# The last feed-forward in groups of two batches, with its convolution as diagonal products on TensorE

## The chip, the cores and the metric

The kernel runs on one core of a Trainium2 chip. A core has five engines that work side by side, each through its own instructions in a fixed order: TensorE (PE; loading its stationary operand is shown apart as PEld), VectorE (DVE), ScalarE (ACT), GpSimd (POOL) and SyncE (SP), which here issues most transfers. They wait for each other by semaphores. PE reads SBUF and writes PSUM, which has eight banks[...]. The metric is the device time of one execution in microseconds (us); the median of several runs is taken.

## The reference

The program is two layers over x of 8 batches x 112 tokens x 256 channels. Each layer adds a cross-attention and a feed-forward to x, both on normalised x. The first feed-forward is a mixture of experts. The second one, which is changed, is a feed-forward with quantised activations and ternary weights, and a convolution of three taps along the tokens:

```python
def act_quant(x):
    scale = 127.0 / jnp.clip(jnp.max(jnp.abs(x), axis=-1, keepdims=True), 1e-05)
    return jnp.clip(jnp.round(x * scale), -128, 127) / scale
...
h = bit_linear(x, w1)                            # 256 -> 1024 channels
h = depthwise_conv1d(h.transpose(0, 2, 1), conv_w, conv_b)
h = h.transpose(0, 2, 1)
h = jax.nn.silu(h)
return bit_linear(h, w2)                         # 1024 -> 256
```

bit_linear quantises its input for each token (act_quant over all channels) and its weight to -1, 0 and 1 times a mean. So the second quantisation needs, for every token, the largest magnitude over 1024 channels after SiLU.

## The kernel before, in words

The kernel is written in a language in which tiles are taken from pools of rotating buffers, and a scheduler orders the instructions of each engine when the program is built, by readiness and by place in the program. All waits are made from the tiles' uses. A pool opened after another was closed takes over its memory.

The stages follow each other: attention of layer 0 with the routing, the experts (to about 449 us), attention of layer 1 (`attention(1, ...)`, L843), and the last feed-forward (L846 to L953). Attention 1 begins with `combine` (L507), which gathers the experts' results by 16 indirect transfers issued on POOL (L511). It ends with `project` for the last batch (L669), whose addition to x (L674) the feed-forward waits for. Attention 1 uses all eight PSUM banks, and its SBUF pools lie where the feed-forward's pools come to lie. The experts' weights were in a pool `wexp` that is closed before attention 1 (L839).

The feed-forward works on two halves of four batches each, 448 tokens (`HT`).

- `quantize_in` (L878): normalises four batches (`ln_apply`, L217), takes each token's largest magnitude (L883), forms scale and step (`quant_scales`, L855), multiplies and clamps (L887, L890), rounds by adding and subtracting a large constant `MAGIC` (L890, L891), transposes on PE (L896) with copies on ACT (L897). The step of each token is laid along the free axis of all partitions by `spread` (L865): a diagonal is made on DVE (L868) and multiplied by ones on PE (L875); dT (L899) is its copy.
- `conv` (L902), once for each of eight blocks of 128 channels (`NF`): two bf16 products (L907) into one bank, h on DVE as product times dT (L911), the middle tap and bias on ACT (L913), the two outer taps on DVE (L914, L917), SiLU on ACT (L920) into `ys`.
- `quantize_out` (L923): the largest magnitude over the eight blocks in one reduction (L925), across the partitions by transposes (L930) and a second reduction (L932), scales, `spread` of the scale, multiplication (L935), clamping (L936), rounding to bf16 (L938), and for each batch eight bf16 products (L943), scaling with the addition of x (L947), and the output transfer on SP's queue (L948).

Both halves' inputs come first, then both convolutions, then both outputs (L950 to L953), unless the scheduler finds an engine free.

Of the kernel before, what the change touches and what calls it, by code (L numbers as in the profile page):

```python
# [12 lines left out]
F32 = mybir.dt.float32  # L13
BF16 = mybir.dt.bfloat16
I32 = mybir.dt.int32
AF = mybir.ActivationFunctionType
ALU = mybir.AluOpType
# [6 lines left out]
H, A = 16, 16  # L24
E, F = 8, 1024
NF = F // 128
HB = B // 2
HT = HB * S
G = 4


# [23 lines left out]
def xattn_ffn_kernel(  # L55
# [17 lines left out]
    def const(shape, name, dt=F32):  # L73
        return cp.tile(shape, dt, tag=name, name=name)
# [28 lines left out]
    def col(name, j=0, n=1):  # L103
        lo = COLS[name][0] + j
        return colt[:, lo : lo + n]
# [49 lines left out]
    vbuf = [kp.tile([KC, NKC, H, 2 * A], F32, tag="v", name="v") for _ in range(3)]  # L155
    for v in vbuf:
        nc.gpsimd.memset(v, 1.0)
    desc = const([128, E], "desc")
    first = const([128, E], "first")
    for e in range(E):  # L160
# [54 lines left out]
    def ln_apply(dst, b, stats):  # L215
        mv, rs = stats
        nc.vector.tensor_scalar(dst, xs[b], mv[:, 0:1], rs, ALU.subtract, ALU.mult)  # L217
# [28 lines left out]
    class Router:  # L246
        def __init__(self, pool, misc, small):
            self.pool, self.misc, self.small = pool, misc, small
            self.cproj = const([128, 2, E], "cproj")
            self.cn = const([128, E], "cn")  # L250
            self.cn1 = const([128, E], "cn1")
# [28 lines left out]
        def norm(self, b, stats):  # L280
            n = self.pool.tile([S, D], F32, tag="r_n", name="rn")
            ln_apply(n, b, stats)
            return n
# [472 lines left out]
    with (  # L756
# [50 lines left out]
        def back(t, hT):  # L807
            w2, b2 = experts[t][1][:, : NF * D].rearrange("p (f d) -> p f d", f=NF), experts[t][1][:, NF * D :]
            py = ps_y.tile([TP, D], F32, tag="y", name="t_y")
            for f in range(NF):  # L810
                nc.tensor.matmul(py, hT[:, f, :], w2[:, f, :], start=(f == 0), stop=(f == NF - 1))  # L811
            y = f3.tile([TP, D], F32, tag="y", name="y")
            nc.vector.tensor_tensor(y, py, b2, ALU.add)  # L813
            return y
# [23 lines left out]

    held.close()  # L839


    stats_f1 = {}
    attention(1, {}, stats_f1)  # L843


    with (  # L846
        tc.tile_pool(name="ffn", bufs=2) as fp,
        tc.tile_pool(name="ffn3", bufs=3) as f3,
        tc.tile_pool(name="ffn1", bufs=1) as f1,
        tc.tile_pool(name="fps_h", bufs=3, space=PSUM) as ps_h,  # L850
        tc.tile_pool(name="fps_y", bufs=2, space=PSUM) as ps_y,
        tc.tile_pool(name="fps_m", bufs=2, space=PSUM) as ps_m,
    ):

        def quant_scales(peak, mean, nb):  # L855

            s = fp.tile([S, nb], F32, tag="qs", name="qs")
            d = fp.tile([S, nb], F32, tag="qd", name="qd")
            nc.vector.tensor_scalar_max(peak, peak, 1e-5)
            nc.vector.reciprocal(s, peak)  # L860
            nc.vector.tensor_scalar_mul(s, s, 127.0)
            nc.vector.tensor_scalar(d, peak, 1.0 / 127.0, mean[:S], ALU.mult, ALU.mult)
            return s, d

        def spread(per_token):  # L865

            dg = fp.tile([S, HB, S], F32, tag="diag", name="diag")
            nc.vector.tensor_tensor(  # L868
                dg,
                ident[:S, :S].unsqueeze(1).to_broadcast([S, HB, S]),  # L870
                per_token.unsqueeze(2).to_broadcast([S, HB, S]),
                ALU.mult,
            )
            t = ps_m.tile([128, HT], F32, tag="m", name="t_sp")
            nc.tensor.matmul(t, ones[:S, :], dg.rearrange("p b s -> p (b s)"), start=True, stop=True)  # L875
            return t

        def quantize_in(i):  # L878
            nall = fp.tile([S, HB, D], F32, tag="nall", name="nall")
            for bb in range(HB):  # L880
                ln_apply(nall[:, bb, :], i * HB + bb, stats_f1[i * HB + bb])
            peak = fp.tile([S, HB], F32, tag="peak", name="peak")
            nc.vector.tensor_reduce(peak, nall, AX.X, ALU.max, apply_absolute_value=True)  # L883
            s, d = quant_scales(peak, w1mean, HB)
            q = fp.tile([S, HB, D], BF16, tag="q16", name="q16")
            for bb in range(HB):
                nc.vector.tensor_scalar(  # L887
                    nall[:, bb, :], nall[:, bb, :], s[:, bb : bb + 1], 127.0, ALU.mult, ALU.min
                )
            nc.vector.tensor_scalar(nall, nall, -128.0, MAGIC, ALU.max, ALU.add)  # L890
            nc.vector.tensor_scalar_sub(q, nall, MAGIC)  # L891
            qT = fp.tile([128, 2, HT], BF16, tag="qT", name="qT")
            for bb in range(HB):
                t = ps_m.tile([128, 2, S], BF16, tag="m", name="t_q")
                for c in range(2):
                    nc.tensor.transpose(t[:, c, :], q[:, bb, c * 128 : (c + 1) * 128], ident16[:S, :S])  # L896
                nc.scalar.copy(qT[:, :, bb * S : (bb + 1) * S], t)  # L897
            dT = fp.tile([128, HT], F32, tag="dT", name="dT")
            nc.vector.tensor_copy(dT, spread(d))  # L899
            return qT, dT  # L900

        def conv(qT, dT):  # L902
            ys = fp.tile([128, NF, HT], F32, tag="ys", name="ys")
            for f in range(NF):
                t = ps_h.tile([128, HT], F32, tag="h", name="t_h")
                for c in range(2):
                    nc.tensor.matmul(  # L907
                        t, w1q[:, c, f * 128 : (f + 1) * 128], qT[:, c, :], start=(c == 0), stop=(c == 1)
                    )
                h = f3.tile([128, HB, S], F32, tag="h", name="h")  # L910
                nc.vector.tensor_tensor(h.rearrange("p b s -> p (b s)"), t, dT, ALU.mult)  # L911
                y = f3.tile([128, HB, S], F32, tag="y", name="y")
                nc.scalar.activation(y, h, AF.Identity, bias=col("cb", f), scale=col("cw", 3 * f + 1))  # L913
                nc.vector.scalar_tensor_tensor(  # L914
                    y[:, :, 1:S], h[:, :, 0 : S - 1], col("cw", 3 * f), y[:, :, 1:S], ALU.mult, ALU.add
                )
                nc.vector.scalar_tensor_tensor(  # L917
                    y[:, :, 0 : S - 1], h[:, :, 1:S], col("cw", 3 * f + 2), y[:, :, 0 : S - 1], ALU.mult, ALU.add
                )
                nc.scalar.activation(ys[:, f, :], y.rearrange("p b s -> p (b s)"), AF.Silu)  # L920
            return ys

        def quantize_out(i, ys):  # L923
            am = fp.tile([128, HT], F32, tag="am", name="am")
            nc.vector.tensor_reduce(  # L925
                am, ys.rearrange("p f t -> p t f"), AX.X, ALU.max, apply_absolute_value=True
            )
            t = ps_m.tile([S, HB, 128], F32, tag="m", name="t_am")
            for bb in range(HB):
                nc.tensor.transpose(t[:, bb, :], am[:, bb * S : (bb + 1) * S], ident)  # L930
            peak = fp.tile([S, HB], F32, tag="peak", name="peak")
            nc.vector.tensor_reduce(peak, t, AX.X, ALU.max)  # L932
            s, d = quant_scales(peak, w2mean, HB)
            sT = spread(s)
            nc.vector.tensor_tensor(ys, ys, sT.unsqueeze(1).to_broadcast([128, NF, HT]), ALU.mult)  # L935
            nc.vector.tensor_scalar(ys, ys, 127.0, -128.0, ALU.min, ALU.max)  # L936
            q = fp.tile([128, NF, HT], BF16, tag="yq", name="yq")
            nc.vector.tensor_scalar(q, ys, MAGIC, MAGIC, ALU.add, ALU.subtract)  # L938
            for bb in range(HB):
                b = i * HB + bb  # L940
                t = ps_y.tile([S, D], F32, tag="y", name="t_y")
                for f in range(NF):
                    nc.tensor.matmul(  # L943
                        t, q[:, f, bb * S : (bb + 1) * S], w2q[:, f, :], start=(f == 0), stop=(f == NF - 1)
                    )
                o = fp.tile([S, D], F32, tag="o", name="o")
                nc.vector.scalar_tensor_tensor(o, t, d[:, bb : bb + 1], xs[b], ALU.mult, ALU.add)  # L947
                nc.sync.dma_start(out=out[b], in_=o)  # L948

        ins = [quantize_in(i) for i in range(2)]  # L950
        ys = [conv(*ins[i]) for i in range(2)]
        for i in range(2):
            quantize_out(i, ys[i])  # L953


_ORDER = [
# [72 lines left out]
```

## Time and profile before

| What | Value |
|---|---|
| Time, median of 3 runs | 776.65 us (776.01 to 777.24) |
| The profiled execution's own time | 783.55 us |
| Its span, first to last instruction | 781.8 us |
| PE, DVE, ACT, POOL busy over the span | 656.6, 461.5, 240.9, 43.2 us |
| Mean granted TensorE clock | 0.862 |
| From 690 us to the end: PE, DVE, ACT busy | 32.3, 76.8, 23.4 us |
| Last x complete (L674 starts) | 690.0 us |
| Last output computed (L947 starts) | 778.2 us |

A group's line reads: line of the kernel, engine, operation, output tile <- input tiles, shapes (partitions x elements; for PE first the rows x columns of the array), count | busy us, mean ns of one | idle us of the engine before them, and what ended most of it. A timeline's line reads: start, duration, engine, line, operation, tiles, count, and in brackets the idle time before. Busy time of PE is modelled at its end, since matmuls are pipelined: several in a row take less than the sum of their means. An fp32 matmul in the program shows as two instructions. The granted clock is TensorE's share of full speed; it is recorded as 0.5 or 1.0, and a mean lies between.

### The profile page before, as it was taken

Reading aid. Unit: us, or ns where it says so; the run is one execution under the profiler, and the core shown is the slowest. Engines: PE = TensorE matmul, PEld = TensorE weight load, DVE = VectorE, ACT = ScalarE, POOL = GpSimd, SP = SyncE. Lnnn points to the kernel's source line nnn. Section 1 sums busy time; section 2 is a strip of 40 time slices with the busy share of each in tenths; the row PEclk is TensorE's granted clock in tenths of the full one; section 3 lists DMA queues with packets and bytes.
Section 4 is the critical chain, followed back from the end, with each engine's and each line's share of the span. In section 5 each row is a group of like instructions: output and inputs, shape, how many; then the busy total and the mean of one; then the engine's idle time right before and its main releaser. Section 6 shows DMA issues by size and latency. Waiting matters only on the chain.

```text
span 781.8 us, 15060 instructions
## 1 busy us (share of the span) xinstructions
PE 656.6 (84%) x5906; PEld 473.8 (61%) x5906; DVE 461.5 (59%) x1664; ACT 240.9 (31%) x476; POOL 43.2 (6%) x83
## 2 busy tenths in 40 slices
PE   4999989999989739999999967999999989845143
PEld 2666666566556529999999844666666656621032
DVE  8855677765763750111011148769887886479975
ACT  1124333233233214433434311133433332317300
POOL 4000000000000110000000061000000000000000
PEclk9999999999688959999999986579999986556558
DMA  9999101002000016979899420000000000000001
GB/s 298 366 344 347 68 2 55 13 14 68 14 13 13 26 57 242 317 279 354 330 328 358 160 83 19 1 2 1 2 2 2 2 1 2 1 1 0 0 10 37
DMA packets 37074, 82.73 MB, mean 106 GB/s; under 512 B 3228, under 2 KB 29196, under 8 KB 31628
## 3 DMA queue, kind: packets, MB, share of 16 engines
q1 hardware_dynamic: 34092, 76.25, 27.7%
q0 software_dynamic: 1536, 3.67, 1.5%
q10 hardware_dynamic: 1376, 1.87, 0.8%
q8 instruction: 46, 0.75, 0.4%
q14 instruction: 24, 0.20, 0.1%
HBM read 61.59 MB, written 20.19 MB: 105 GB/s over the span
## 4 chain that ended last, share of the span: by engine, by line
PE 66%; DVE 20%; DMA 6%; issue 4%; ACT 2%; SPq 1%; POOL 0%; another core or an unknown queue 0%; POOLq 0%; DVEq 0%; ACTq 0%
PE t_k L229 10%; PE t_h L800 10%; PE t_y L811 9%; PE t_p L618 7%; PE sc L585 7%; PE po L640 5%; PE t_v L236 4%; PE t_q L535 4%; DMA tok<-rn,at 2%; PE t_out L673 2%; DVE am L925 2%; PE t_o L652 2%; DVE a L198 1%; DVE top L588 1%; PE t_y L943 1%
## 5 line engine op out<-in xcount | busy, mean ns | idle before, releaser
L229 PE MATMUL t_k<-ctx,wk 128*128 128x375 f32 x256 | 96.3, 520 | 4.3 <-DMA ctx<-in_ctxT_dram 3.5
L800 PE MATMUL t_h<-tnT,we 128*128 128x128 f32 x672 | 92.1, 281 | 0.5 <-DMA we<-in_WA_dram 0.3
L800 PEld LDWEIGHTS t_h<-tnT,we 128*128 128x128 f32 x672 | 87.8, 194 | 7.4 <-ACT hT L804 1.6
L585 PE MATMUL sc<-k,q 32*112 32x375 f32 x512 | 86.9, 576 | 4.4 <-DVE pT L628 2.3
L804 ACT ACTIVATE hT<-t_h,we 128x128 f32<-128x128 f32 x168 | 61.4, 368 | 91.9 <-PE t_h L800 86.4
L811 PE MATMUL t_y<-we,hT 128*128 128x256 f32 x336 | 82.8, 380 | 0.0
L618 PE MATMUL t_p<-qa,k 32*125 32x112 f32 x1536 | 78.9, 315 | 2.9 <-DVE top L588 1.5
L630 ACT ACTIVATE pT<-pT 125x672 f32<-125x672 f32 x64 | 48.8, 763 | 105.5 <-DVE pT L628 103.4
L618 PEld LDWEIGHTS t_p<-qa,k 32*125 32x125 f32 x1536 | 62.6, 209 | 20.8 <-issue 14.0
L588 DVE TENSOR_REDUCE top<-sc 112x2 f32<-112x750 f32 x64 | 57.9, 933 | 26.7 <-PE sc L585 26.6
L229 PEld LDWEIGHTS t_k<-ctx,wk 128*128 128x128 f32 x256 | 49.1, 203 | 35.3 <-issue 6.1
L630 ACT ACTIVATE pT<-t_p 125x672 f32<-125x672 f32 x64 | 43.3, 728 | 86.0 <-PE t_p L618 85.9
L628 DVE TENSOR_TENSOR pT<-t_p,maskT 125x336 f32<-125x336 f32 x128 | 56.6, 499 | 21.4 <-PE t_p L618 21.4
L595 DVE CUSTOM_DVE_ANT_0 sm<-sc,mask 112x375 f32<-112x375 f32 x128 | 63.0, 541 | 9.8 <-PE sc L585 9.7
L640 PE MATMUL po<-pT,v 125*32 125x112 f32 x1536 | 62.4, 288 | 6.7 <-ACT pT L630 4.3
L811 PEld LDWEIGHTS t_y<-we,hT 128*128 128x128 f32 x336 | 59.1, 191 | 5.5
L640 PEld LDWEIGHTS po<-pT,v 125*32 125x32 f32 x1536 | 41.1, 119 | 31.3 <-ACT pT L630 13.5
L789 DVE COPY tnT<-t_tn 128x256 f32<-128x256 f32 x21 | 8.9, 425 | 78.0 <-PE t_tn L787 70.7
L813 DVE TENSOR_TENSOR y<-t_y,we 128x256 f32<-128x256 f32 x21 | 8.9, 424 | 68.9 <-PE t_y L811 68.8
L585 PEld LDWEIGHTS sc<-k,q 32*112 32x112 f32 x512 | 29.1, 189 | 31.5 <-issue 17.0
L236 PE MATMUL t_v<-wv,ctx 128*125 128x256 f32 x192 | 45.9, 387 | 0.3 <-ACT k L558 0.3
L535 PE MATMUL t_q<-nT,wq 128*128 128x112 f32 x256 | 37.7, 308 | 3.1 <-DVE qa L608 2.5
(207 smaller groups left out, 772.4 us busy)
## 6 DMA issues: line engine op xcount, KB each, us to landing
we<-in_WB_dram SPq DMA_DIRECT2D x21, 1152.0 KB, 7.8
we<-in_WA_dram SPq DMA_DIRECT2D x21, 1028.0 KB, 6.6
tok<-zero SPq DMA_DIRECT2D x8, 896.0 KB, 9.7
ysc<-zero SPq DMA_DIRECT2D x8, 896.0 KB, 10.7
ctx<-in_ctxT_dram SPq DMA_DIRECT2D x8, 375.0 KB, 7.3
tn<-tok SPq DMA_DIRECT2D x21, 128.0 KB, 7.0
ysc<-y SPq DMA_DIRECT2D x21, 128.0 KB, 3.6
we<-in_w1T_dram SPq DMA_DIRECT2D x1, 1024.0 KB, 9.3
```

The lines of the kernel that those rows point to most:

```text
L229: nc.tensor.matmul(t, wts[layer]["k"][:, c, g * 128 : (g + 1) * 128], ctx_t[b][:, c, :], start=(c == 0), stop=(c == 1),)
L236: nc.tensor.matmul(t, ctx_t[b][:, c, i * KC : (i + 1) * KC], wts[layer]["v"][:, c, :], start=(c == 0), stop=(c == 1),)
L535: nc.tensor.matmul(t[:, g, :], wts[layer]["q"][:, c, g * 128 : (g + 1) * 128], nT[:, c, :], start=(c == 0), stop=(c == 1),)
L585: nc.tensor.matmul(ts[j // 2][:S, j % 2, :SK], q[r, g, :], k[r, g, :], start=True, stop=True)
L588: nc.vector.tensor_reduce(top[:, g, 2 * m : 2 * m + 2, A : A + 1], ts[m][:S, :, :SK], AX.X, ALU.max, negate=True,)
L595: nc.vector.tensor_tensor_reduce(out=sm, in0=ts[m][:S, i, :SK], in1=mask_t, scale=-1.0, scalar=3.0e38, op0=ALU.add, op1=ALU.min, accum_out ...
L618: nc.tensor.matmul(ts[j // 2][:KC, j % 2, c * S : (c + 1) * S], k[r, g, c * KC : (c + 1) * KC], qa[r, g, :], start=True, stop=True,)
L630: nc.scalar.activation(pT, src, AF.Exp)
L640: nc.tensor.matmul(po[32 * j : 32 * j + 32, g, :], v[:, c, 4 * g + j, :], pTs[j // 2][:, j % 2, c * S : (c + 1) * S], start=(c == 0), stop ...
L800: nc.tensor.matmul(ph[:, i, :], w1[:, c, f * 128 : (f + 1) * 128], nt[:, c, :], start=(c == 0), stop=(c == 1),)
L804: nc.scalar.activation(hT[:, f, :], ph[:, i, :], AF.Gelu, bias=b1[:, f : f + 1])
L811: nc.tensor.matmul(py, hT[:, f, :], w2[:, f, :], start=(f == 0), stop=(f == NF - 1))
```

## The change

The feed-forward is put into a class `Ffn` that works on four groups of two batches (`GB` = 2, 224 tokens, `GT`), with its own tiles.

- Input: `norm`, `quant` and `turn_in` do for two batches what `quantize_in` did for four. Clamps are left out; scaling and adding `MAGIC` are one DVE instruction, and subtracting it with rounding to bf16 is an ACT instruction (`minus_magic` as bias). dT is copied on ACT. The diagonals of `spread` are made on POOL.
- Convolution: for two channel blocks at once, four bf16 products fill one bank, and DVE writes h into one of three padded buffers `hpad` (zeros at both ends of each batch). Each tap is then an fp32 product of a 128x128 diagonal matrix of tap weights (`taps`) with the shifted h, three adding up in PSUM for each block, 96 in all. ACT applies SiLU with the convolution's bias straight from PSUM.
- Largest magnitude: ACT takes Abs of each pair of blocks, DVE keeps a running maximum; `peaks` finishes it.
- Output: `back` is as before without clamping, for two batches, and is placed within the next group's convolution.
- `late`, called after attention 1 in the program, fills `hpad` with zeros and makes `taps` on POOL. Their pool is opened before attention 1, in the memory of `wexp`.
- PSUM: two banks for first products (`ps_h`), three for taps (`ps_c`), three for the rest (`ps_m`).

```diff
-HB = B // 2
-HT = HB * S
+GB = 2
+GT, NGR = GB * S, B // GB
...
+    minus_magic = const([128, 1], "mmagic")
+    nc.gpsimd.memset(minus_magic, -MAGIC)
...
+    lp = ctx.enter_context(tc.tile_pool(name="late", bufs=1))
+    hpad = [lp.tile([128, 2, GB, S + 2], F32, tag=f"hpad{i}", name=f"hpad{i}") for i in range(3)]
+    taps = lp.tile([128, NF * 3, 128], F32, tag="taps", name="taps")
+
+    def late():
+        for t in hpad:
+            nc.gpsimd.memset(t, 0.0)
+        for f in range(NF):
+            nc.gpsimd.tensor_tensor(
+                taps[:, 3 * f : 3 * f + 3, :],
+                ident.unsqueeze(1).to_broadcast([128, 3, 128]),
+                col("cw", 3 * f, 3).unsqueeze(2).to_broadcast([128, 3, 128]),
+                ALU.mult,
+            )
...
     attention(1, {}, stats_f1)
+    late()
...
-        tc.tile_pool(name="fps_h", bufs=3, space=PSUM) as ps_h,
-        tc.tile_pool(name="fps_y", bufs=2, space=PSUM) as ps_y,
-        tc.tile_pool(name="fps_m", bufs=2, space=PSUM) as ps_m,
+        tc.tile_pool(name="fps_h", bufs=2, space=PSUM) as ps_h,
+        tc.tile_pool(name="fps_c", bufs=3, space=PSUM) as ps_c,
+        tc.tile_pool(name="fps_m", bufs=3, space=PSUM) as ps_m,
...
+            def spread(self, per_token):
+                e = self.p2.tile([S, GB, S], F32, tag="diag", name="diag")
+                nc.gpsimd.tensor_tensor(
+                    e,
+                    ident[:S, :S].unsqueeze(1).to_broadcast([S, GB, S]),
+                    per_token.unsqueeze(2).to_broadcast([S, GB, S]),
+                    ALU.mult,
                 )
+                t = self.bank_m("t_sp")[:, :GT]
+                nc.tensor.matmul(t, ones[:S, :], e.rearrange("p b s -> p (b s)"), start=True, stop=True)
+                return t
...
+            def quant(self, g):
+                n = self.st[g].pop("n")
+                peak = self.p2.tile([S, GB], F32, tag="peak", name="peak")
+                nc.vector.tensor_reduce(peak, n, AX.X, ALU.max, apply_absolute_value=True)
+                s, d = self.scales(peak, w1mean)
+                q = self.p2.tile([S, GB, D], BF16, tag="q16", name="q16")
+                for bb in range(GB):
+                    nc.vector.tensor_scalar(n[:, bb, :], n[:, bb, :], s[:, bb : bb + 1], MAGIC, ALU.mult, ALU.add)
+                nc.scalar.activation(q, n, AF.Identity, bias=minus_magic[:S])
+                self.st[g]["q"], self.st[g]["d"] = q, d
...
+            def conv(self, g, fp, silu):
...
+                t = self.bank_h("t_h")[:, : 2 * GT].rearrange("p (i n) -> p i n", i=2)
+                for i in range(2):
+                    f = 2 * fp + i
+                    for c in range(2):
+                        nc.tensor.matmul(
+                            t[:, i, :], w1q[:, c, f * 128 : (f + 1) * 128], st["qT"][:, c, :],
+                            start=(c == 0), stop=(c == 1),
+                        )
+                h = hpad[self.turn % 3]
+                self.turn += 1
+                nc.vector.tensor_tensor(
+                    h[:, :, :, 1 : S + 1], t.rearrange("p i (b s) -> p i b s", b=GB),
+                    st["dT"].rearrange("p (b s) -> p b s", b=GB).unsqueeze(1).to_broadcast([128, 2, GB, S]),
+                    ALU.mult,
+                )
+                y = self.bank_c("t_c")[:, : 2 * GT].rearrange("p (i b s) -> p i b s", i=2, b=GB)
+                for i in range(2):
+                    f = 2 * fp + i
+                    for j in range(3):
+                        nc.tensor.matmul(
+                            y[:, i], taps[:, 3 * f + j, :], h[:, i, :, j : j + S], start=(j == 0), stop=(j == 2)
+                        )
+                for i in range(2):
+                    f = 2 * fp + i
+                    nc.scalar.activation(
+                        st["ys"][:, f, :].rearrange("p (b s) -> p b s", b=GB), y[:, i],
+                        AF.Silu if silu else AF.Identity, bias=col("cb", f),
                     )
+                if silu:
+                    self.magnitudes(g, fp)
+
+            def magnitudes(self, g, fp):
+                st = self.st[g]
+                ys = st["ys"][:, 2 * fp : 2 * fp + 2, :]
+                a = self.p2.tile([128, 2, GT], F32, tag="am" if fp == 0 else "ab", name="am")
+                nc.scalar.activation(a, ys, AF.Abs)
+                if fp == 0:
+                    st["am"] = a
+                else:
+                    nc.vector.tensor_tensor(st["am"], st["am"], a, ALU.max)
...
+            def peaks(self, g):
+                m = self.st[g].pop("am")
+                nc.vector.tensor_tensor(m[:, 0], m[:, 0], m[:, 1], ALU.max)
+                t = self.bank_m("t_am")[:S, : GB * 128].rearrange("s (b p) -> s b p", b=GB)
+                for bb in range(GB):
+                    nc.tensor.transpose(t[:, bb, :], m[:, 0, bb * S : (bb + 1) * S], ident)
+                peak = self.p2.tile([S, GB], F32, tag="peak", name="peak")
+                nc.vector.tensor_reduce(peak, t, AX.X, ALU.max)
+                s, self.st[g]["d"] = self.scales(peak, w2mean)
+                self.st[g]["sT"] = self.spread(s)
+
+            def back(self, g):
+                st = self.st[g]
+                ys = st.pop("ys")
+                nc.vector.tensor_tensor(ys, ys, st.pop("sT").unsqueeze(1).to_broadcast([128, NF, GT]), ALU.mult)
+                q = self.p2.tile([128, NF, GT], BF16, tag="yq", name="yq")
+                nc.vector.tensor_scalar(q, ys, MAGIC, MAGIC, ALU.add, ALU.subtract)
...
+        begin(0)
+        for g in range(NGR):
+            for f in range(NF // 2):
+                ff.conv(g, f, True)
+                if f == 1 and g + 1 < NGR:
+                    begin(g + 1)
+                if f == 2 and g > 0:
+                    ff.back(g - 1)
+            ff.peaks(g)
+        ff.back(NGR - 1)
```

`begin(g)` calls `norm` for both batches, `quant` and `turn_in`.

## The prediction

> **What bounds the stage now.** I read the profile from the end backwards: first the chain of waits of the last 92 us, then the instruction groups of that stretch, then TensorE's clock, and last the single instructions at its two ends. The page's whole-kernel shares (PE 84% busy) say nothing about this stage.
>
> ```profile
> by line: issue 17.4%; DVE am L925 13.3%; PE t_y L943 10.6%; DVE y L914 9.3%; DVE y L917 7.4%; DVE h L911 6.4%; PE t_sp L875 6.0%; DVE yq L938 4.4%; DVE ys L935 4.3%; DVE ys L936 4.2%; PE t_h L907 2.6%; DMA out_dram<-o 2.0%; ACT qT L897 1.7%
> ```
>
> That is the chain in 690 to 782 us. It runs through VectorE (DVE) nearly all the way; where PE stands on it (t_y, t_sp), DVE is waiting with nothing else to do.
>
> ```profile
> L925 DVE TENSOR_REDUCE am<-ys 128x448 f32<-128x3584 f32 x2 | 12.4, 6176 | 0.1
> L907 PE MATMUL t_h<-qT,w0q 128*128 128x448 bf16 x32 | 12.2, 507 | 10.6 <-DVE h L911 10.6
> L943 PE MATMUL t_y<-w1q,yq 128*112 128x256 bf16 x64 | 11.5, 363 | 16.1 <-DVE yq L938 16.1
> L917 DVE SCALAR_TENSOR_TENSOR y<-h,cols,y 128x444 f32<-128x444 f32 x16 | 10.4, 670 | 0.0
> L914 DVE SCALAR_TENSOR_TENSOR y<-h,cols,y 128x444 f32<-128x444 f32 x16 | 10.4, 669 | 0.0
> L911 DVE TENSOR_TENSOR h<-t_h,dT 128x448 f32<-128x448 f32 x16 | 9.5, 613 | 0.0
> L920 ACT ACTIVATE ys<-y 128x448 f32<-128x448 f32 x16 | 9.0, 571 | 10.6 <-DVE y L917 10.6
> L935 DVE TENSOR_TENSOR ys<-ys,t_sp 128x3584 f32<-128x3584 f32 x2 | 7.8, 3888 | 3.1 <-PE t_sp L875 3.1
> ```
>
> The groups of the same stretch: DVE's rows have no idle time before them, PE's and ACT's wait for DVE. DVE is busy for 76.8 us of these 92.
>
> ```profile
> 640.00:656.00 16.00, 16.00 (x150) 9.37 (x146) 9.97 (x32) 4.47 (x7) 0.00 (x0) 0.50 0.01 2
> 712.00:756.00 44.00, 10.73 (x26) 4.05 (x26) 41.88 (x49) 14.80 (x24) 0.00 (x0) 0.50 0.00 0
> 300.00:440.00 140.00, 139.63 (x932) 128.77 (x932) 15.71 (x37) 53.68 (x146) 0.00 (x0) 1.00 0.90 328
> ```
>
> Busy time by stretch (PE, weight loads, DVE, ACT, POOL, then PE's granted clock). In the stage PE works a quarter of the time at half clock; in the experts (300 to 440) full-size fp32 products keep it at 1.00; at 640 it is busy throughout and still gets 0.50.
>
> ```profile
> 399.82 1.70 PEld L811 LDWEIGHTS t_y<-we,hT 128*128 128x128 f32 x8
> 690.00 0.42 DVE L674 TENSOR_TENSOR x<-t_out,x 112x256 f32<-112x256 f32 x1 [3.27 <-PE t_out L673]
> 703.24 0.62 DVE L911 TENSOR_TENSOR h<-t_h,dT 128x448 f32<-128x448 f32 x1
> 706.36 1.02 PE L875 MATMUL t_sp<-diag,ones 112*128 112x448 f32 x2 [0.40 <-ACT qT L897]
> 756.85 6.12 PE L943 MATMUL t_y<-w1q,yq 128*112 128x256 bf16 x32 [7.72 <-DVE yq L938]
> 778.21 0.48 DVE L947 SCALAR_TENSOR_TENSOR o<-t_y,qd,x 112x256 f32<-112x256 f32 x1 [1.14 <-DMA out_dram<-o]
> ```
>
> The timeline: the stage can begin at 690.0, when the last batch's x is complete; its first h is made 13.2 us later; the last output is made at 778.7, 3.1 us before the end. The first line gives PE's price for fp32 at full clock: eight products of 256 columns in 1.70 us, 213 ns each, and a written fp32 matmul is two such instructions. So one fp32 matmul costs 1.66 ns a column, and a bf16 one a quarter; t_sp (448 columns, 2 instructions in 1.02 us with its latency) agrees.
>
> **The change, engine by engine.** *DVE.* Removed: the two tap additions (10.4 + 10.4), the reduction over channels (12.4), both clamps (L936 4.0, and one of three passes over n), diag and dT (3.7). Added: running maxima, 12 of 128x448 at 0.61 (L911's row) and 4 of half that. Per group of two batches: 4 h and 3 maxima at 0.61 = 4.3; normalising 2.9 (2 x 0.40, reduce 0.69, four small at 0.17, 2 x 0.35); peaks 1.5; back 4.1 (half of 3888, half of 2026, 2 x 0.48). Sum 12.8, four groups 51 us. DVE stops being the bound.
>
> *ACT.* Identity with a bias costs 355 ns at 112 columns and 571 at 375 (attention's rows), so SiLU on 224 is about 0.45: 32 of them 14.2; 16 magnitudes at 0.57 (L920's row) 9.1; input rounding, qT and dT 1.6 a group. About 30 us, beside other work. *Abs* is in no row. [...] The trace shows that for Identity and Copy alone: one 1.28 us load before the first SiLU and none after. [...] otherwise each of 16 pairs adds two, 41 us, and ACT's 68 us would be the bound. [...]
>
> *PE.* Added: 4 groups x 8 channel blocks x 3 taps = 96 fp32 products of 224 columns, at 0.373 us: 35.8 us at full clock, 71.7 at half. The rest at full clock: 64 first products of 224 bf16 columns at 0.10 = 6.4; 64 last ones at 0.107 = 6.9; 8 spreads at 0.37 = 3.0; transposes 1.7. Sum 54 us: **PE is the new bound**, closely ahead of DVE, and its clock decides.
>
> [...] The row of 640 to 656 shows 16 us of PE "busy" at 0.50. [...] by that row 72, and the change loses. [...] at 640 the products are 32 rows by 112 columns[...]; the experts' 128x128 fp32 products hold 1.00 for 140 us, and 32 t_y in a row at 756.85 bring the clock back within their 6.1 us. The taps are of the experts' kind. I charge one start at half clock, about 5 us long: 2.5 lost.
>
> *POOL.* It gets the 8 diagonals of 224 columns (L522: 726 ns for 256, so 0.66), on the path only in the last group, and before attention 1 the tap tables and padding: 8 x 1.0 + 3 x 0.47 = 9.4 us on a queue that then issues 16 gathers (L511, 936 ns each, the first at 451.97). Their memory is that of the expert weights, so they start between about 441 and 449. They may fit into idle POOL time (0) or stand ahead of the first gather, on which combine, normalisation and the first scores wait (up to 6.6). I take 1: they stand behind the gathers in the program, so that only gaps should be given to them. SP's eight output transfers remain; six now leave before the tail, and the wait for an output buffer at the end (1.14) goes.
>
> **The sum on the path**, on the profiled execution's own span:
> - Start. x at 690.0; two normalisations, reduce, scales, scaling on DVE to 693.6; rounding on ACT 0.72; four transposes 0.5, copy 0.53, four products at half clock 0.95, h 0.6, hops 0.3: first tap at 697.2. Before, the first h came at 703.2, because four batches were prepared in seven passes.
> - PE from there: 54 less what the start (1.2) and the tail (2.3) hold: 50.4, plus 2.5 for the cold start.
> - Waits of PE. It has two banks of first products; the taps of a pair stand ahead of later first products in program order, so I expect PE to issue two first products, wait for one h, and then run two pairs. That is 8 waits of about 0.9 (h 0.6 and half of a DVE instruction in front). I take 7 us. Lower end 0 (first products always early enough), upper 20 (below).
> - Tail after the last tap: two SiLU 0.9, Abs 0.57, two maxima 1.0, transposes 0.6, reduce 0.42, scales 0.45, diagonal on POOL 0.7, spread at half clock 0.95, scaling 2.0, rounding 1.03, 16 t_y at half clock 3.1, output 0.5, the 3.1 to the end, hops 0.5: 15.8.
>
> 697.2 + 50.4 + 2.5 + 7 + 15.8 = 772.9, plus POOL's 1: 773.9 against 781.8, **7.9 us less**. The profiled execution took 783.55, 6.9 above the median of the runs; I carry the difference over, not the ratio: 776.65 - 7.9 = **768.7**.
>
> **Rivals.**
> - *PE never waits* (first products always issued early): 7 us better, 761. For it: DVE is busy for only some 42 of the 60 us, ACT for 27. Against: DVE works in written order, and back's 3.1 us stand before some h.
> - *PE waits for h in every pair* (the slower one): the place is the wait of a tap product for h behind DVE's scaling and rounding (2.0 + 1.03, in three groups) and behind a maximum. 16 x 0.7 + 3 x 3.0 = 20, so 782. It decides from 15 us on, 0.93 us a pair. For it: in the profile before, the reduction at 730.84 (6.18 us) was put ahead of the last two tap additions, which then waited.
> - *The clock stays at half*: PE's 50.4 more, less the 2.5 and some 5 of waits: 812. It turns the sign once about 8 us of PE's full-clock work run at half. Against: above.
> - *Abs reloads tables*: ACT's 68 us in place of PE's 60, with more waits: 777 to 785.
> - *Nothing gained because another engine binds*: it would need DVE at 60 us or more; its rows give 51.
>
> **How the numbers follow.** Forecast case 0.66 (own range 763 to 775), no waits 0.12, waits in every pair 0.12, half clock 0.06, Abs 0.04. From 760 to 779.5 the range holds the first two cases and the better part of the third; half clock, the worse waits and part of Abs, about 0.19, are left out. A measurement of this kernel tells 0.2%, 1.6 us, from no change. Faster: nearly all of the first two, 0.78; same: a part of waits and of Abs, 0.06; slower: the rest, 0.16.
>
> **What will show it.** Right: PE's clock near 1.00 from about 702 to 755, 192 tap records following each other at 0.19 us, h's rows without long gaps, first tap near 697, one table load. Wrong if the clock row shows 0.5 in the stage, if PE's waits for h exceed 15 us, if more than one table load stands between SiLUs, or if the first gather moves to after 453.

## The result, and the profile after

The changed kernel takes 768.18 us (median; 764.19 to 771.66) against 776.94 for the kernel before: a ratio of 0.9881 with a 95% interval of 0.9834 to 0.9928, 8.8 us less. The prediction said 768.7 and 7.9 us less. A second measurement, further down, gave 0.9894 (0.9843 to 0.9945). The profiles of the kernel before and of the later version "first products ahead" come from slower executions (783.55 and 764.07 us); the ratios leave such executions out and need not equal the quotient of two medians.

Attention 1 takes a different time in each execution: between the experts' last y and the last x, the twelve profiles of this study lie between 233 and 242 us. Within it the versions differ only in POOL's tables, which ten of them make at its start, and in the feed-forward's early work on DVE near its end. I therefore compare the **stage** in the profiles: from the start of the last addition to x to the end of the span. It was 91.8 us and is 79.0. Where the same feed-forward was profiled twice, the stage repeats to 0.4 us: 91.8 and 91.4 for the one before, 79.0 and 79.1 for the changed one.

Chain of waits of the changed kernel in 670 to 770 us (the view ends the line there):

```profile
by line: PE t_c L960 29.3%; PE t_y L1011 9.3%; DVE ys L1003 8.1%; PE t_p L620 5.7%; PE po L642 4.9%; PE t_out L675 4.0%; PE t_sp L902 3.5%; DVE yq L1005 3.3%; DVE hpad L951 3.1%; PE t_h L945 3.1%; issue 2.8%; DVE nall L918 2.2%; DVE peak L9
```

Where DVE's additions and its reduction stood, PE's taps (t_c) stand now. Instruction groups of the changed kernel, 680 to 770 us:

```profile
L960 PE MATMUL t_c<-hpad,taps 128*128 128x224 f32 x192 | 40.4, 359 | 2.0 <-DVE hpad L951 2.0
L965 ACT ACTIVATE ys<-t_c,cols 128x224 f32<-128x224 f32 x32 | 12.6, 443 | 31.2 <-PE t_c L960 31.2
L951 DVE TENSOR_TENSOR hpad<-t_h,dT 128x448 f32<-128x448 f32 x16 | 9.4, 618 | 8.1 <-PE t_h L945 8.1
L977 ACT ACTIVATE am<-ys 128x448 f32<-128x448 f32 x16 | 9.3, 579 | 0.4
L981 DVE TENSOR_TENSOR am<-am 128x448 f32<-128x448 f32 x12 | 7.4, 619 | 6.6 <-ACT am L977 6.6
L965 ACT ACT_TABLE_LOAD x1 | 1.3, 1283 | 0.0
```

The roles are exchanged: DVE and ACT now have idle time in front of their rows and wait for PE, and t_c waits for hardly anything. There is one table load (1.28 us), so the 16 Abs added none. Busy time of the changed kernel by stretch (first tap to last tap, then the tail), and of the kernel before from its last x on:

```profile
695.34:753.43 58.09, 53.47 (x321) 48.87 (x319) 35.28 (x76) 24.61 (x53) 2.81 (x5) 0.99 0.04 13
753.43:769.90 16.47, 5.18 (x20) 3.94 (x20) 6.06 (x11) 1.36 (x3) 0.56 (x1) 0.65 0.05 14
```

```profile
690.00:781.80 91.80, 32.32 (x128) 19.15 (x128) 76.78 (x123) 23.35 (x41) 0.00 (x0) 0.61 0.04 10
```

PE is busy for 53.5 of 58.1 us at a granted clock of 0.99; DVE has fallen from 76.8 us to 45.1 over the whole stage. The timeline of the changed kernel shows the pieces of the sum:

```profile
685.09 1.06 DVE L219 TENSOR_SCALAR nall<-x,mv,rs 112x256 f32<-112x256 f32 x3 [2.37 <-PE po L642]
690.94 0.42 DVE L676 TENSOR_TENSOR x<-t_out,x 112x256 f32<-112x256 f32 x1 [1.41 <-PE t_out L675]
695.34 5.42 PE L960 MATMUL t_c<-hpad,taps 128*128 128x224 f32 x24
700.59 0.93 PE L945 MATMUL t_h<-qT,w0q 128*128 128x224 bf16 x8
701.25 1.16 DVE L951 TENSOR_TENSOR hpad<-t_h,dT 128x448 f32<-128x448 f32 x2 [4.34 <-PE t_h L945]
701.93 4.81 PE L960 MATMUL t_c<-hpad,taps 128*128 128x224 f32 x24 [0.41 <-DVE hpad L951]
706.57 0.93 PE L945 MATMUL t_h<-qT,w0q 128*128 128x224 bf16 x8
766.34 0.48 DVE L1015 SCALAR_TENSOR_TENSOR o<-t_y,qd,x 112x256 f32<-112x256 f32 x1 [1.22 <-PE t_y L1011]
```

Normalising the first group begins 5.9 us before the last x is complete. Then PE's pattern: two pairs' first products (8 matmuls), a wait of 0.4 us for h, the taps of two pairs (24 instructions) in 4.8 us, and again.

### The profile page after: what moved, and what is told of

Its sections match the earlier page's. It is cut to its first block, busy times and chain, and to the rows that moved or that the text cites. A ratio compares the mean times of both kernels' runs of the same rounds, so it can differ in the third digit from the quotient of the medians.

```text
span 769.9 us, 15569 instructions
## 1 busy us (share of the span) xinstructions
PE 684.9 (89%) x6138; PEld 511.2 (66%) x6138; DVE 436.7 (57%) x1658; ACT 246.0 (32%) x496; POOL 55.7 (7%) x103
## 4 chain that ended last, share of the span: by engine, by line
PE 50%; DVE 7%; DMA 2%; issue 1%; POOL 1%; ACT 0%; SPq 0%; POOLq 0%; DVEq 0%; ACTq 0%
PE t_h L802 10%; PE t_y L813 9%; PE sc L587 6%; PE t_p L620 5%; PE po L642 4%; PE t_c L960 4%; PE t_k L231 4%; PE t_q L537 2%; PE t_v L238 2%; PE t_y L1011 1%; PE t_out L675 1%; DVE ys L1003 1%; DVE pT L630 1%; DMA we<-in_WA_dram 1%; PE t_o L654 1%
## 5 line engine op out<-in xcount | busy, mean ns | idle before, releaser
L642 PE MATMUL po<-pT,v 125*32 125x112 f32 x1536 | 64.0, 291 | 6.6 <-ACT pT L632 4.2
L537 PE MATMUL t_q<-nT,wq 128*128 128x112 f32 x256 | 39.4, 317 | 5.2 <-DVE qa L610 4.6
```

The lines of the kernel that those rows point to most:

```text
L642: nc.tensor.matmul(po[32 * j : 32 * j + 32, g, :], v[:, c, 4 * g + j, :], pTs[j // 2][:, j % 2, c * S : (c + 1) * S], start=(c == 0), stop ...
```

## The experiments

The theory was the prediction's: the stage was bound by DVE, is now bound by PE, and DVE has room. The rival that came to matter is that the move of the taps brings nothing, and the gain has other parts. All runs, with the stage of each one's profile (in the edits below, lines are joined, and "..." stands for what is left out):

| Version | Taps on | Magnitudes | Tokens a group | Stage, us | Time, us | Ratio to before (95%) |
|---|---|---|---|---|---|---|
| before | DVE, ACT | DVE reduction | 448 | 91.8 | 772.9 to 776.9 | 1 |
| changed | PE, fp32 | ACT, DVE maximum | 224 | 79.0 | 768.18 | 0.9881 (0.9834 to 0.9928) |
| changed, again | the same | the same | 224 | 79.1 | 765.44 | 0.9894 (0.9843 to 0.9945) |
| tables alone | DVE, ACT | DVE reduction | 448 | 91.4 | 776.41 | 1.0002 (0.9968 to 1.0035) |
| magnitudes only | DVE, ACT | ACT, DVE maximum | 448 | 86.1 | 771.99 | 0.9890 (0.9791 to 0.9988) |
| groups only | DVE, ACT | DVE reduction | 224 | 85.0 | 770.47 | 0.9936 (0.9913 to 0.9958) |
| convolution on DVE | DVE, ACT | ACT, DVE maximum | 224 | 78.7 | 764.17 | 0.9872 (0.9825 to 0.9920) |
| maximum on DVE | PE, fp32 | DVE reduction | 224 | 84.2 | 769.47 | 0.9918 (0.9886 to 0.9950) |
| taps in bf16 | PE, bf16 | ACT, DVE maximum | 224 | 61.3 | 747.09 | 0.9622 (0.9568 to 0.9676) |
| first products ahead | PE, fp32 | ACT, DVE maximum | 224 | 74.7 | 755.67 | 0.9674 (0.9577 to 0.9771) |
| bf16 and ahead | PE, bf16 | ACT, DVE maximum | 224 | 63.1 | 749.71 | 0.9588 (0.9484 to 0.9692) |
| one pair in four on DVE | both, fp32 | ACT, DVE maximum | 224 | 67.4 | 755.07 | 0.9753 (0.9685 to 0.9820) |

**Does PE bind the convolution?** Taps and padded h in bf16; the rounding of h is then coarser than the reference's computation.

```diff
-    hpad = [lp.tile([128, 2, GB, S + 2], F32, ...
-    taps = lp.tile([128, NF * 3, 128], F32, ...
+    hpad = [lp.tile([128, 2, GB, S + 2], BF16, ...
+    taps = lp.tile([128, NF * 3, 128], BF16, ...
```

> The changed kernel with taps and padded h in bf16, so that a tap costs a quarter on TensorE; h is rounded more coarsely than the reference asks. Theory (TensorE binds the convolution stretch of 58 us): TensorE's work there falls by 27 us, VectorE's 35 us plus its waits take over, the time falls by 8 to 14 us, to 754 to 760; if the granted clock drops to half [...], by 3 to 8. Rival (the handshake with VectorE already sets the pace): less than 3 us.

Measured: 747.09 us. The stage falls by 17.7 us and the time by 21.1, more than expected. The first to last tap of this version:

```profile
691.12:725.61 34.49, 26.73 (x207) 21.82 (x205) 28.77 (x67) 22.18 (x52) 2.82 (x4) 0.87 0.05 14
```

PE's work in the stretch falls by 26.7 us (192 instructions at 0.189 us apiece, less three quarters, would be 27.2, an estimate), and the stretch from 58.1 to 34.5; the tail grows from 16.5 to 22.4, because part of an earlier group's output now falls behind the last tap. PE did bind. With cheap taps PE is busy for 26.7 and DVE for 28.8 of the 34.5 us, at a granted clock of 0.87. My size was too small because I took DVE's 35 us for a floor: 28.8 us of DVE's work lie in the shorter stretch, the rest around it.

**Is it the taps on PE that pay?** The rest as changed, the convolution as before but for two blocks of 224 tokens:

```diff
-                        nc.tensor.matmul(y[:, i], taps[:, 3 * f + j, :], h[:, i, :, j : j + S], ...)
+                    nc.scalar.activation(y[:, i], h[:, i], AF.Identity, bias=col("cb", f), scale=col("cw", 3 * f + 1))
+                    nc.vector.scalar_tensor_tensor(y[:, i, :, 1:S], h[:, i, :, 0 : S - 1], col("cw", 3 * f), ...)
+                    nc.vector.scalar_tensor_tensor(y[:, i, :, 0 : S - 1], h[:, i, :, 1:S], col("cw", 3 * f + 2), ...)
...
+                nc.scalar.activation(st["ys"][:, 2 * fp : 2 * fp + 2, :], y..., AF.Silu)
```

With it, h lies in rotating buffers without padding, and SiLU takes a pair of blocks in one instruction.

> The changed kernel in groups of two, with the middle tap and bias on ScalarE and the outer taps on VectorE as before; magnitudes, running maximum and everything else as changed. Theory (the gain comes from taking the taps off VectorE): VectorE gets 28 us more and binds again, the stage from the last x to the end is 86 to 92 us, the time 774 to 780. Rival (the gain is the smaller groups, that start earlier and overlap): the time stays within 3 us of the changed kernel's 768.

Measured: 764.17 us and a stage of 78.7, a clear miss of my theory. The rival is nearer: the time is 4.0 us below the changed kernel's 768.18 and 1.3 below its second measurement. Without a single diagonal product the stage is as short as with them. Groups of this version:

```profile
L965 DVE SCALAR_TENSOR_TENSOR y<-h,cols,y 128x222 f32<-128x222 f32 x32 | 13.5, 441 | 0.0
L962 DVE SCALAR_TENSOR_TENSOR y<-h,cols,y 128x222 f32<-128x222 f32 x32 | 13.5, 442 | 0.7 <-ACT y L959 0.7
L946 PE MATMUL t_h<-qT,w0q 128*128 128x224 bf16 x64 | 12.1, 343 | 10.2 <-DVE h L951 10.2
```

```profile
683.34:762.00 78.66, 36.76 (x168) 26.90 (x166) 65.79 (x165) 39.13 (x76) 3.71 (x6) 0.61 0.04 12
```

```profile
689.93 0.80 DVE L962 SCALAR_TENSOR_TENSOR y<-h,cols,y 128x222 f32<-128x222 f32 x2
690.65 0.80 DVE L965 SCALAR_TENSOR_TENSOR y<-h,cols,y 128x222 f32<-128x222 f32 x2
```

DVE's additions have no idle time before them and PE waits for h: DVE binds again. But it is busy for 65.8 us, 20.7 more than in the changed kernel and not 28: following each other the additions start 0.36 us apart, though each lasts 0.44, and I had counted durations. PE meanwhile runs at a granted clock of 0.61 and still waits for DVE.

**What are the other two parts worth?** One reduction for each group in place of the 16 Abs and 12 maxima, with taps on PE:

```diff
-                if silu:
-                    self.magnitudes(g, fp)
...
-                m = self.st[g].pop("am")
-                nc.vector.tensor_tensor(m[:, 0], m[:, 0], m[:, 1], ALU.max)
+                m = self.p2.tile([128, 1, GT], F32, tag="am", name="am")
+                nc.vector.tensor_reduce(m[:, 0], self.st[g]["ys"].rearrange("p f t -> p t f"), AX.X, ALU.max, apply_absolute_value=True)
```

> The changed kernel with one VectorE reduction over the eight blocks of a group in place of ScalarE's magnitudes and the running maximum. Theory (VectorE has room in the convolution, only the last group's is on the path): tail longer by 1.3 us (3.1 in place of Abs 0.58, maxima 1.0 and their hops), and some waits of TensorE for h behind the 3.1 us reduction; 1 to 5 us slower than the changed kernel, 769 to 773. Rival (VectorE's load matters everywhere): 8 us or more slower, no gain left over the kernel before.

Measured: 769.47 us, stage 84.2, 5.2 longer. The first and the last of the four reductions in the timeline, and PE's wait for h in the list of waits (us in total, times, longest):

```profile
697.69 3.25 DVE L989 TENSOR_REDUCE am<-ys 128x224 f32<-128x1792 f32 x1
747.94 3.16 DVE L989 TENSOR_REDUCE am<-ys 128x224 f32<-128x1792 f32 x1 [2.61 <-ACT ys L965]
```

```profile
PE t_c L960 <- DVE hpad L951: 4.8, 10, 1.2
```

The tail grows by 1.5 us and the stretch of the taps by 3.7 (58.1 to 61.8): behind reductions like the one at 697.69, h comes late and PE waits 4.8 us for it in place of 2.0. So DVE's load still matters through PE's waits, though DVE is not the bound, as the expectation had it.

The same step in the kernel before, in halves, was tried alone:

```diff
                 nc.scalar.activation(ys[:, f, :], y.rearrange("p b s -> p (b s)"), AF.Silu)
...
+                    nc.scalar.activation(ab, ys[:, f, :], AF.Abs)
+                    nc.vector.tensor_tensor(am, am, ab, ALU.max)
...
-            nc.vector.tensor_reduce(am, ys.rearrange("p f t -> p t f"), AX.X, ALU.max, apply_absolute_value=True)
```

> The kernel before, in halves of four batches, with ScalarE's Abs of each block and a running maximum on VectorE in place of the two reductions; nothing else. Theory (VectorE-bound): reductions 12.4 become 14 maxima of about 0.54 = 7.6, and the convolution's last additions no longer stand behind a reduction of 6.2 us: stage 91.8 falls to 84 to 88. Rival (ScalarE's 9 us more make VectorE wait as much): 90 to 92.

Measured: 771.99 us, stage 86.1: 5.7 us less, as the theory had it (the medians differ by 3.6: 775.60 to 771.99). And groups of two alone, which is the version with the convolution on DVE plus the reduction above:

> Groups of two with taps on ScalarE and VectorE and the largest magnitude as one VectorE reduction a group: neither diagonals nor Abs. Theory (with VectorE bound, each of its instructions counts at its pitch): stage 78.7 of the run with the convolution on VectorE, plus four reductions of 3.1, less maxima of 7.7: 83 to 85 us from last x to end, so that groups, dropped clamps and POOL's diagonals alone bring 7 to 9 us over the kernel before (91.8). Rival (groups bring nothing without the magnitudes): 89 to 92.

Measured: 770.47 us, stage 85.0: 6.8 us less, just under the 7 to 9 that were expected.

```profile
686.91:771.90 84.99, 35.98 (x168) 26.71 (x166) 71.25 (x153) 31.15 (x60) 3.70 (x6) 0.62 0.04 11
```

In this run the tables are still made, clamps are dropped, the diagonals of the spreads are on POOL and dT is copied on ACT, so these go with "groups". DVE is busy for 71.3 us of the stage where it was for 76.8, 5.5 less: work that is gone, or that lies ahead of the last x now. In the kernel before, the clamp of L936 (4.0), the diagonals (2.5) and the copies of dT (1.2) alone take 7.7. What the smaller groups bring without these was not tried.

The parts add up: groups 6.8 and magnitudes 5.7 make 12.5 of the 13.1 us that the version without diagonals gains in the stage. The diagonals add -0.3 with magnitudes on ACT (78.7 to 79.0) and +0.8 without (85.0 to 84.2): next to nothing, against a repeat of 0.1 to 0.4. This holds for fp32 taps in this order of instructions. With bf16 taps, above, the stage is 17.4 us below the 78.7 of the version on DVE, and with fp32 taps in the order of the next experiment it is 4.0 below. Whether that order would shorten the version on DVE too was not tried.

**Where are PE's remaining waits?** First products and h one pair earlier in the program:

```diff
+        ff.first(*pairs[0])
+        for n, (g, f) in enumerate(pairs):
+            if n + 1 < len(pairs):
+                ff.first(*pairs[n + 1])
             ff.conv(g, f, True)
...
```

> The changed kernel with each pair's first products and h placed one pair earlier in the program, nothing else. Theory (TensorE binds, and its 4.6 us of idle time in the 58.1 us from the first to the last tap are waits for h after every second pair and for VectorE's and POOL's results): the waits for h go, the stretch falls to 54 to 56 us, the stage from last x to end from 79.0 to 75 to 77. Rival (the waits move to the next late thing, VectorE's rounded output or the diagonals): stage within 1 us of 79.0.

Measured: 755.67 us against 775.60 for the kernel before beside it; first to last tap 53.6 us, stage 74.7. That stretch and PE's timeline in it:

```profile
692.06:745.66 53.60, 52.93 (x321) 48.45 (x319) 36.08 (x76) 24.91 (x53) 2.81 (x5) 0.98 0.04 11
```

```profile
697.90 0.55 PE L945 MATMUL t_h<-qT,w0q 128*128 128x224 bf16 x4
698.28 2.45 PE L966 MATMUL t_c<-hpad,taps 128*128 128x224 f32 x12
700.57 0.55 PE L945 MATMUL t_h<-qT,w0q 128*128 128x224 bf16 x4
700.95 2.45 PE L966 MATMUL t_c<-hpad,taps 128*128 128x224 f32 x12
```

Four first products and one pair's taps alternate without a wait, and PE is busy for 52.9 of the 53.6 us. The wait for h was the order's doing, as the prediction's step had it. In bf16 the same step was tried too:

> Taps and h in bf16, with first products one pair earlier. Theory (without the taps' cost nothing is bound in the middle; VectorE 35 of 44 us and TensorE wait for each other in written order): stage 61.3 of the bf16 run falls by 0 to 3 us. Rival (order set by first products): by more than 3 us.

Measured: 749.71 us and a stage of 63.1, where 61.3 stood without it: a miss, since nothing was gained. Here, where PE is not the only bound, its order gave nothing; what sets those 61 us I did not settle.

**Does sharing the taps pay?** If each engine alone is the bound with all taps, each should be relieved by giving some away. In the version with first products ahead, the second of the four pairs takes its taps on ACT and DVE, the others as before:

```diff
+                if fp == 1:
...
+                        nc.scalar.activation(y[:, i], h[:, i, :, 1 : S + 1], AF.Identity, bias=col("cb", f), scale=col("cw", 3 * f + 1))
+                        for j in (0, 2):
+                            nc.vector.scalar_tensor_tensor(y[:, i], h[:, i, :, j : j + S], col("cw", 3 * f + j), y[:, i], ...)
...
+                else:
...
```

> The version with first products one pair ahead, in which one of a group's four pairs takes its taps on ScalarE and VectorE and the other three on TensorE, all in fp32. Theory (taps cost the stage the same on either engine because each then binds it alone, so sharing them is what pays): TensorE's work falls by 4 x 2.3 = 9 us, VectorE's rises from 36 to about 42 in the stretch; stage from 74.7 to 66 to 71. Rival (waits between the engines fill what is freed): 73 to 76.

Measured: 755.07 us against 772.89 for the kernel before beside it. The stage is 67.4, 7.3 less than with all taps on PE in the same order. First to last tap:

```profile
690.13:736.81 46.68, 42.98 (x257) 38.35 (x255) 38.17 (x90) 27.25 (x57) 2.87 (x5) 0.98 0.04 11
```

PE 43.0 and DVE 38.2 of 46.7 us: both are now used, and of the versions that keep fp32 this one has the shortest stage. The time does not confirm it: 755.07 us here and 755.67 without the sharing, which are 17.8 and 19.9 us less than the kernel before of the same measurement, and the intervals of the two ratios overlap. So the 7.3 us rest on one profile of each version, and a gain in time from sharing is not shown. With bf16 taps the time is shorter than in both, 747.09.

**What do the tables cost?** The kernel before with nothing but paddings and tables on POOL:

```diff
     attention(1, {}, stats_f1)
+    late()
```

> The kernel before, with only the padding and tap tables made on POOL at the start of attention 1; nothing reads them. Theory (attention 1 is later bound by TensorE and swallows the delay): the first gather moves about 2 us later after the last y, the last x of attention 1 by less than 0.5 us, time within 0.2% of before. Rival (the start of attention 1 is on the path): the time rises by the same 2 us, 0.25%.

Measured: 776.41 us, ratio 1.0002 (0.9968 to 1.0035). POOL in the changed kernel at that place:

```profile
450.59 1.32 POOL L849 MEMSET hpad<- 128x456 f32 x3 [164.06 <-DVE y L815]
451.87 3.18 POOL L851 TENSOR_TENSOR taps<-ident,cols 128x384 f32<-128x384 f32 x4
455.21 0.98 POOL L513 DMA_INDIRECT yg<-ysc,at  x1 [0.16 <-issue]
```

Four tables and the padding stand before the first gather. It starts 4.69 us after the last y is done, where it started 2.75 after: 1.9 us later. With the tables alone the gather is as late (4.68), yet from the last y to the last x that profile has 240.5 us, where the kernel before has 240.8: the delay is not to be seen there. The interval of the time is wide enough to hold 0 as well as these 1.9, so that question stays open.

**The changed kernel again:**

> The changed kernel unaltered, once more beside the kernel before. If the profiles' difference of the stage (91.8 to 79.0) is the whole effect, the ratio is near 0.9835; if 3 to 4 us of it are lost elsewhere (the start of attention 1 behind POOL's tables), near 0.988; the stage in its profile is 78.5 to 80 us either way.

Measured: 765.44 us, ratio 0.9894; stage 79.1. Both measurements gain less in the median (8.8 and 7.5 us) than the profiles' stages differ by (12.7 to 12.8). The two profiled executions differ by 11.9 (783.55 and 771.66). POOL's 1.9 us could be part of what is missing, though no profile shows it. The rest the runs don't explain: the last x is complete anywhere between 680.9 and 690.9 us in the twelve profiles, so the start of the stage varies by more than that from one execution to the next.

## Why the prediction was right, step by step

*The number* was right, and so was the move of the bound from DVE to PE. But two errors of some 4 us with opposite signs meet in the number, which is luck, and the gain does not come from where the prediction sought it.

- *PE becomes the bound, at full clock*: right. Estimated after the first tap: 50.4 of work, 2.5 for the cold start, 7 of waits, together 59.9; measured 58.1, of which 53.5 busy. The price of a tap held: back to back, the instructions start 0.189 us apart in the median at full clock, where 0.187 was taken, and 0.374 in the 1.4 us at half. So did the quarter for bf16: in the kernel before, at full clock, 256 columns take 0.109 us in bf16 (L943) and twice 0.216 in fp32 (L811). The clock was at half for only the first 1.4 us, up to 696.78, which costs 0.7 in place of 2.5; so PE's work at full clock was about 52.8, some 2.4 more than estimated.
- *Clock of the taps*: the prediction set the 0.50 at 640 us beside the experts' 1.00 and took the taps to be of the experts' kind. They ran so: 0.99 in this stretch, 1.00 from 696.78 to 758.22. That the kind of product decides was the author's estimate from those two stretches; no run varied it alone.
- *Waits of PE*: the pattern (two first products, one wait, two pairs) is as described, 4.6 us of idle time in place of 7; the version with first products ahead has 4.5 us less in the stretch.
- *Start*: 7.2 us from the last x to the first tap were estimated, 4.4 measured. The term assumed, from the kernel before, that nothing of the stage can begin until the last x is there. In the changed kernel normalising the first group starts at 685.09, released by attention's last po. This is the one term that was mis-sized in kind.
- *Tail*: 15.8 estimated, 16.5 measured. The clock fell to half at 758.22, just before the spread, so that the spread and the last products ran at half as assumed: t_y's instructions start 0.213 us apart there, and 0.109 at full clock.
- *Abs*: that it adds no table load was the author's assumption; it held. The changed kernel's trace has four loads of 1.28 us in all, as many as that of the kernel before, and one of them in the stage.
- *POOL*: taken as 1 because "only gaps should be given to them". That was wrong: the padding and four tables went before the gathers, and the first gather came at 455.21, past the 453 that the prediction named as a sign of error. The last y was 1.3 us later in this profile; the delay itself is 1.9 us, with an unresolved effect on the time.
- *The whole*: from the last x to the end 82.9 predicted (772.9 - 690.0), 79.0 measured; against it stand the 4 us by which the medians gain less than the stage. The estimate hit the median because these two cancel.
- *Readings*: "DVE's rows have no idle time before them" is not so for L935, which waits 3.1 us for the spread, and `back`'s three parts make 3.9 a group and not 4.1. Neither changes the sum.

What the prediction left unasked is which part of the change pays. DVE's busy time, 51 us by its count, came to 45.1 in the stage, and PE's 54 to 53.5 between the first and the last tap; but it did not compare this with leaving the taps where they were. Counted at their spacing, DVE's taps add only 20.7 us, the DVE-bound stage is 78.7, and PE's 58 us plus start and tail make 79.0. The gain is that of the magnitudes and of the groups with all that goes with them, not of the taps.

Of the rivals, half clock and Abs did not occur. PE did not wait in every pair. What it does almost without waits, the version with first products ahead shows: a stage of 74.7.

## What to carry to other kernels

When a change moves work to another engine and does other things as well, price the version with everything but the move: here it has all of the gain. Count instructions of a busy engine at their spacing, not at their duration, since back to back these DVE additions took 0.36 us and not 0.44. Where two engines price the same work alike, sharing it between them is worth trying: one pair in four moved back shortened the profiled stage by 7.3 us, though the time did not follow.

## What the runs showed of the hardware

The recorded clock of PE is 0.5 or 1.0. In the traces of the kernels before and after, the stretches at one clock (27 and 19, without the last of each) take 3.41 us or a multiple of it: in the kernel before half from 662.84 to 703.80 us (40.96), full to 710.63 (6.83), half to 761.83 (51.20), full to 768.65 (6.83). Where instructions of one kind follow each other, they start this far apart (median):

| Instruction | Kernel | At half clock, us | At full clock, us |
|---|---|---|---|
| bf16, 224 columns (t_h, L945) | changed | 0.187 | 0.096 |
| bf16, 256 columns (t_y, L943) | before | 0.213 | 0.109 |
| fp32, 224 columns (taps, L960) | changed | 0.374 | 0.189 |
| fp32, 256 columns (t_out, L673) | before | 0.427 | 0.216 |

An fp32 product takes two of its instructions (192 for 96 taps). PE's busy time and mean clock in stretches of four traces:

| Kernel, stretch in us | PE busy, us | Mostly | Clock |
|---|---|---|---|
| before, 300 to 440 | 139.6 of 140 | the experts' fp32 products, 128x128 | 1.00 |
| before, 520 to 620 | 100.0 of 100 | sc, t_p, po (920 of 1174 instructions) beside 128x128 | 1.00 |
| before, 640 to 656 | 16.0 of 16 | sc, t_p, po (140 of 150 instructions) | 0.50 |
| before, 712 to 756 | 10.7 of 44 | first products of the convolution | 0.50 |
| changed, 696.4 to 757 | 52.8 of 60.6 | fp32 taps, 128x128 | 1.00 |
| bf16 taps, 691.1 to 725.6 | 26.7 of 34.5 | bf16 taps, 128x128 | 0.87 |
| convolution on DVE, 683.3 to 762 | 36.8 of 78.7 | bf16 products | 0.61 |

sc, t_p and po work on 32 rows or 32 columns. The busy time alone does not tell the clock: 16.0 of 16 us went with 0.50, and 52.8 of 60.6 with 1.00. What decides it was not shown.
